# The nine taps of a depthwise convolution divided anew among four engines, and one of its outputs stored turned

## The chip, the core and the metric

The kernel runs on one core of a Trainium2 chip. The core has five engines that each work through their own queue in order: TensorE (PE, matmuls and transposes), VectorE (DVE), ScalarE (ACT), GpSimd (POOL) and SyncE (SP, which here only issues transfers). Transfers run on 16 DMA engines; a transfer is issued by an instruction in the queue of SP or ACT. TensorE writes to PSUM, which ScalarE and VectorE read. The metric is device time in microseconds, the median of several runs.

## What is computed

The reference has two layers over an image x of 256 x 256 tokens with 128 channels. The first is attention along rows; the change doesn't touch it. The second, cut to what matters (g is the group-normalised input, b is 1, the inner width 256, four scan directions k, 16 states):

```python
xz = g @ w_in.T
xi, z = jnp.split(xz, 2, axis=-1)
xc = transpose(xi, (0, 3, 1, 2))
xc = silu(depthwise_conv_3x3(xc, conv_w) + conv_b)
x_flat = xc.reshape(b, d, L)
x_t = transpose(xc, (0, 1, 3, 2)).reshape(b, d, L)
xs = concatenate([[x_flat, x_t], flip([x_flat, x_t])])
x_dbl = einsum('bkdl,kcd->bkcl', xs, x_proj_w)
dts, Bs, Cs = split(x_dbl, [8, 24], axis=2)
ys = selective_scan(xs, dt_w @ dts, -exp(A_logs), Bs, Cs, Ds, dt_b)
out = x + (layernorm(sum of the four directions of ys) * silu(z)) @ w_out.T
```

So for each token the second layer needs nine multiply-adds in each of 256 channels (the depthwise convolution), a silu, and three small projections: the input of the rates and the C of each direction, B of each direction, and the skip product Ds * xs. Directions 1 and 3 go through the image column by column, so they need their rates and C with the image turned.

## The kernel before

The stages run one after the other: `group_stats`, `pair_norm`, `attention`, `conv`, `swap`, `scans`, `output`. Between them everything goes through scratch tensors in DRAM (`mid_...` in the profile). The change lies in `conv` and in the call of `swap`.

`conv` goes over 32 blocks of 8 image rows (2048 tokens). For each block it loads `raw` (10 rows, SP), makes the normalised frame `pad` with a border of zeros (L506, VectorE; borders by GpSimd, L500 to L505), and projects it into `xi`, 256 channels as two halves h of 128 partitions (L522 on TensorE, ten matmuls of 512 columns; L525 copies each from PSUM on ScalarE).

Each block is four chunks q of 512 tokens. For each chunk and half, four of the nine taps (`corners`) are matmuls into one PSUM tile `ps` (L537): the tap's weights are multiplied into the projection `w_in` once, at the start (L475), so that such a tap reads `pad` and not `xi`. The other five taps (`others`) are VectorE operations that multiply a shifted piece of `xi` by a weight for each partition and add what is there already (L547; the first adds to `ps`, the others to `acc`). Then come the sigmoid on ScalarE (L556) and the product of silu on VectorE (L557), which gives `xc`.

From `xc` a chunk makes: `pd` (L560, two matmuls: rates and C of all four directions in 96 rows), copied to `dc` by ScalarE (L563); `pb` (L567, eight matmuls: B), copied to `bk` by VectorE (L570); `pt` (L574, eight transposes: the tokens), copied to `xk` by ScalarE (L575) and multiplied by the skip weights into `y0` by VectorE (L576). `pd`, `pb` and `pt` have one PSUM buffer each, `ps` three, shared with the projections.

At the end of a block, eight stores stand in ScalarE's queue: `xk`, `y`, the two halves of `dc` (`dc1` for the directions that run across, `dc0` for the others), and four of `bk`, one for each direction (L577 to L582). In a store of `bk` each contiguous run is 16 numbers, 64 bytes. The order of the work in `conv` is not written out by hand; a scheduler puts it into the engines' queues.

`swap` then turns `dc1` into `dcT`: two rounds of eight loads (L598, SP), eight copies that exchange the two image axes (L606 on ScalarE, L608 on VectorE) and sixteen stores (L610, ScalarE's queue).

`scans` reads `dc0` for directions 0 and 2, which come first, and `dcT` for directions 1 and 3. For each state and half it runs a scan on VectorE (L858), multiplies the result by C on GpSimd (L861), and does the rest on TensorE and ScalarE. L659 is its first VectorE operation. In `output`, the last stage, GpSimd multiplies two tiles (L1046) while VectorE normalises (L1019, L1023, L1030).

Of the kernel before, what the change touches and what calls it, by code (L numbers as in the profile page):

```python
# [28 lines left out]
F32 = mybir.dt.float32  # L29
# [6 lines left out]
P = 128  # L36
N = 256
# [417 lines left out]
def conv(tc, io, c):  # L455

    nc = tc.nc
# [3 lines left out]
    corners = (0, 2, 6, 8)  # L463
    others = (1, 3, 4, 5, 7)
    with tc.tile_pool(name="d_w", bufs=1) as wp, tc.tile_pool(name="d_in", bufs=2) as inp, tc.tile_pool(
        name="d_sb", bufs=2
    ) as sb, tc.tile_pool(name="d_out", bufs=2) as op, tc.tile_pool(name="d_ps", bufs=3, space=PSUM) as psum, tc.tile_pool(
# [4 lines left out]
        w4 = wp.tile([P, 4, DI], F32, name="w4")  # L472
        for x, t in enumerate(corners):
            nc.sync.dma_start(out=w4[:, x, :], in_=io["conv_wT"][t].partition_broadcast(P))
        nc.vector.tensor_tensor(w4, w4, bcast(win, 1, [P, 4, DI]), ALU.mult)  # L475
# [14 lines left out]
        for b in range(N // R):  # L490
            toks = slice(b * RT, (b + 1) * RT)
            lo, hi = max(b * R - 1, 0), min(b * R + R + 1, N)
            off = lo - (b * R - 1)
            raw = inp.tile([P, R + 2, N], F32, name="raw")
            rows = hi - lo
            nc.sync.dma_start(
                out=raw[:, off : off + rows, :].rearrange("p r w -> p (r w)"), in_=io["x1T"][:, lo * N : hi * N]
            )
            pad = inp.tile([P, R + 2, N + 2], F32, name="pad")
            nc.gpsimd.memset(pad[:, :, 0:1], 0.0)  # L500
            nc.gpsimd.memset(pad[:, :, N + 1 : N + 2], 0.0)
            if off:
                nc.gpsimd.memset(pad[:, 0, :], 0.0)
            if off + rows < R + 2:
                nc.gpsimd.memset(pad[:, R + 1, :], 0.0)  # L505
            nc.vector.tensor_scalar(  # L506
                pad[:, off : off + rows, 1 : N + 1],
                raw[:, off : off + rows, :],
                c.gn2[:, 0:1],
                c.gn2[:, 1:2],  # L510
                ALU.subtract,
                ALU.mult,
            )
            rr = T // N
            xi = inp.tile([P, NH, R + 2, N + 2], F32, name="xi")
            nc.gpsimd.memset(xi[:, :, :, 0:1], 0.0)
            nc.gpsimd.memset(xi[:, :, :, N + 1 : N + 2], 0.0)
            for r in range(0, R + 2, rr):
                for h in range(NH):
                    rows = min(rr, R + 2 - r)  # L520
                    pi = psum.tile([P, T], F32, name="ps").rearrange("p (r w) -> p r w", w=N)[:, 0:rows, :]
                    nc.tensor.matmul(  # L522
                        pi, win[:, h * P : (h + 1) * P], pad[:, r : r + rows, 1 : N + 1], start=True, stop=True
                    )
                    nc.scalar.copy(xi[:, h, r : r + rows, 1 : N + 1], pi)  # L525
            xk = op.tile([P, RT // P, DI], F32, name="xk")
            y0 = op.tile([P, RT // P, DI], F32, name="y0")
            bk = op.tile([P, KD, RT // P, DS], F32, name="bk")
            dc = op.tile([P, RT], F32, name="dc")
            for q in range(RT // T):  # L530
                qs = slice(q * QJ, (q + 1) * QJ)
                xc = sb.tile([P, NH, T], F32, name="xc")
                for h in range(NH):
                    ps = psum.tile([P, T], F32, name="ps")
                    for x, t in enumerate(corners):
                        dy, dx = divmod(t, 3)
                        nc.tensor.matmul(  # L537
                            ps.rearrange("p (r w) -> p r w", w=N),
                            w4[:, x, h * P : (h + 1) * P],
                            pad[:, q * rr + dy : q * rr + dy + rr, dx : dx + N],  # L540
                            start=(x == 0),
                            stop=(x == len(corners) - 1),
                        )
                    acc = sb.tile([P, T], F32, name="acc")
                    for x, t in enumerate(others):
                        dy, dx = divmod(t, 3)
                        nc.vector.scalar_tensor_tensor(  # L547
                            acc.rearrange("p (r w) -> p r w", w=N),
                            xi[:, h, q * rr + dy : q * rr + dy + rr, dx : dx + N],
                            cw[:, t, h : h + 1],  # L550
                            (acc if x else ps).rearrange("p (r w) -> p r w", w=N),
                            ALU.mult,
                            ALU.add,
                        )
                    sg = sb.tile([P, T], F32, name="sg")
                    nc.scalar.activation(sg, acc, AF.Sigmoid, bias=cb[:, h : h + 1])  # L556
                    nc.vector.scalar_tensor_tensor(xc[:, h, :], acc, cb[:, h : h + 1], sg, ALU.add, ALU.mult)  # L557
                pd = pdp.tile([P, T], F32, name="pd")
                for h in range(NH):
                    nc.tensor.matmul(  # L560
                        pd[0 : KD * RC, :], xpc[:, h, :], xc[:, h, :], start=(h == 0), stop=(h == NH - 1)
                    )
                nc.scalar.copy(dc[0 : KD * RC, q * T : (q + 1) * T], pd[0 : KD * RC, :])  # L563
                pb = pdp.tile([P, QJ, KD * DS], F32, name="pb")
                for j in range(QJ):
                    for h in range(NH):
                        nc.tensor.matmul(  # L567
                            pb[:, j, :], xc[:, h, j * P : (j + 1) * P], xpb[:, h, :], start=(h == 0), stop=(h == NH - 1)
                        )
                nc.vector.tensor_copy(bk[:, :, qs, :].rearrange("p k j n -> p j k n"), pb.rearrange("p j (k n) -> p j k n", n=DS))  # L570
                pt = pdp.tile([P, QJ, DI], F32, name="pt")
                for j in range(QJ):
                    for h in range(NH):
                        nc.tensor.transpose(pt[:, j, h * P : (h + 1) * P], xc[:, h, j * P : (j + 1) * P], c.ident)  # L574
                nc.scalar.copy(xk[:, qs, :], pt)  # L575
                nc.vector.tensor_tensor(y0[:, qs, :], pt, bcast(sk, 1, [P, QJ, DI]), ALU.mult)  # L576
            nc.scalar.dma_start(out=io["xk"][toks, :].rearrange("(j p) c -> p j c", p=P), in_=xk)  # L577
            nc.scalar.dma_start(out=io["y"][toks, :].rearrange("(j p) c -> p j c", p=P), in_=y0)
            nc.scalar.dma_start(out=io["dc1"][:, toks], in_=dc[0 : KD // 2 * RC, :])
            nc.scalar.dma_start(out=io["dc0"][:, toks], in_=dc[KD // 2 * RC : KD * RC, :])  # L580
            for k in range(KD):
                nc.scalar.dma_start(out=io["bk"][k, toks, :].rearrange("(j p) n -> p j n", p=P), in_=bk[:, k])  # L582


def swap(tc, io, src, dst):

    nc = tc.nc
    B = 128
    Q = 16
    PR = KD // 2 * RC  # L590
    s = io[src].rearrange("p (i h w) -> i p h w", h=B, w=N)
    d = io[dst].rearrange("p (w i h) -> i p w h", i=N // B, h=B)
    with tc.tile_pool(name=f"s_{dst}", bufs=1) as sb:
        for j in range(N // B):
            a = sb.tile([P, B, B], F32, name="a")
            for i in range(N // B):
                for q in range(0, B, B // 4):
                    nc.sync.dma_start(  # L598
                        out=a[i * PR : (i + 1) * PR, q : q + B // 4, :],
                        in_=s[i, :, q : q + B // 4, j * B : (j + 1) * B],  # L600
                    )
            o = sb.tile([P, B, B], F32, name="o")
            for n, q in enumerate(range(0, B, Q)):
                to, of = o[0 : N // B * PR, q : q + Q, :], a[0 : N // B * PR, :, q : q + Q].rearrange("p h w -> p w h")
                if n % 2:
                    nc.scalar.copy(to, of)  # L606
                else:
                    nc.vector.tensor_copy(to, of)  # L608
# [385 lines left out]
def output(tc, io, c):  # L994
# [70 lines left out]
    "xk": (NT, DI),  # L1065
    "bk": (KD, NT, DS),
    "dc0": (KD // 2 * RC, NT),
    "dc1": (KD // 2 * RC, NT),
    "dcT": (KD // 2 * RC, NT),
    "y": (NT, DI),  # L1070
}
# [58 lines left out]
```

## Time and profile before

| what | us |
|---|---|
| median of three runs | 28848.39 (28846.53 to 28851.29) |
| the profiled execution | 28855.02 |
| its span in the profile | 28853.2 |
| first frame of the convolution, L506 | starts at 2589.9 |
| last skip product of the convolution, L576 | starts at 4562.3 |
| first load and last store of the swap, L598 and L610 | issued at 4582.5 and 4735.5 |
| first scan, L858 | starts at 4784.3 |

| group in the convolution | count | busy us | mean ns |
|---|---|---|---|
| L537 PE tap matmuls | x2048 | 954.9 | 610 |
| L522 PE projections | x640 | 298.0 | 600 |
| L560 PE rates and C | x512 | 302.3 | 689 |
| L567 PE B | x2048 | 260.0 | 274 |
| L574 PE transposes | x1024 | 150.6 | 275 |
| L547 DVE taps, on acc | x1024 | 754.4 | 749 |
| L547 DVE taps, on ps | x256 | 187.9 | 743 |
| L557 DVE silu | x256 | 189.4 | 749 |
| L576 DVE skip product | x128 | 156.3 | 1221 |
| L506 DVE frame | x32 | 53.5 | 1673 |
| L525 ACT copy to xi | x320 | 187.0 | 586 |
| L556 ACT sigmoid | x256 | 181.7 | 721 |
| L575 ACT copy to xk | x128 | 129.5 | 1012 |
| L563 ACT copy to dc | x128 | 74.5 | 582 |

How to read it: a time in the profile counts from the start of the span. L547 is line 547 of the kernel, `acc<-xi,cw,acc` says that the tile `acc` is written from `xi`, `cw` and `acc`. A matmul of 512 columns in float32 has two records. Records on an engine may overlap a little, so the distance from start to start (the pitch) can be shorter than a record. In a wait, "17.58 <-DMA mid_bk<-bk" says that the engine sat idle for 17.58 us until that transfer's issue or end let it go on. The granted clock is the share of full speed that TensorE was given.

### The profile page before, as it was taken

Reading aid. Unit: us, or ns where it says so; the run is one execution under the profiler, and the core shown is the slowest. Engines: PE = TensorE matmul, PEld = TensorE weight load, DVE = VectorE, ACT = ScalarE, POOL = GpSimd, SP = SyncE. Lnnn points to the kernel's source line nnn. Section 1 sums busy time; section 2 is a strip of 40 time slices with the busy share of each in tenths; the row PEclk is TensorE's granted clock in tenths of the full one; section 3 lists DMA queues with packets and bytes.
Section 4 is the critical chain, followed back from the end, with each engine's and each line's share of the span. In section 5 each row is a group of like instructions: output and inputs, shape, how many; then the busy total and the mean of one; then the engine's idle time right before and its main releaser. Section 6 shows DMA issues by size and latency. Waiting matters only on the chain. (4 is left out here: it accounts for less than half of the span.)

```text
span 28853.2 us, 534744 instructions
## 1 busy us (share of the span) xinstructions
PE 26874.7 (93%) x196490; PEld 22493.7 (78%) x196490; DVE 25687.9 (89%) x28349; ACT 25335.6 (88%) x49673; POOL 23024.8 (80%) x10118
## 2 busy tenths in 40 slices
PE   8999996999999999999999999999999999999998
PEld 3555444888888888888888888888888888888884
DVE  4777665999999999999999999999999999999997
ACT  6885225999999999999999999999999999999987
POOL 2442003999999999999999999999999999999983
PEclk9999998999999999999999999999999999999999
DMA  5112444333333333333333333333333333333335
GB/s 204 54 54 70 114 114 115 130 130 128 129 128 130 130 130 130 130 129 130 127 131 130 129 130 130 129 130 127 130 130 130 130 128 129 128 128 130 130 129 173
DMA packets 1924048, 3630.49 MB, mean 126 GB/s; under 512 B 532297, under 2 KB 1240009, under 8 KB 1889490
## 3 DMA queue, kind: packets, MB, share of 16 engines
q1 hardware_dynamic: 1424722, 3339.77, 34.1%
q10 hardware_dynamic: 496640, 255.88, 3.2%
q8 instruction: 1567, 25.67, 0.4%
q14 instruction: 1119, 9.17, 0.1%
HBM read 3002.42 MB, written 592.84 MB: 125 GB/s over the span
## 5 line engine op out<-in xcount | busy, mean ns | idle before, releaser
L861 POOL TENSOR_TENSOR hs<-hs,cc 128x1024 f32<-128x1024 f32 x8192 | 19304.2, 2375 | 1669.6 <-DVE state L860 1178.4
L858 DVE TENSOR_TENSOR_SCAN hs<-da,state,mm 128x1024 f32<-128x1024 f32 x8192 | 19223.4, 2347 | 1026.0 <-PE mm L848 697.5
L846 PE MATMUL mm<-dg,dxt 128*128 128x128 f32 x65536 | 9412.3, 288 | 1260.4 <-DVE hs L858 1023.7
L846 PEld LDWEIGHTS mm<-dg,dxt 128*128 128x128 f32 x65536 | 8243.5, 197 | 2746.4 <-DVE hs L858 2084.1
L839 ACT ACTIVATE da<-delta,A 128x1024 f32<-128x1024 f32 x8192 | 9342.1, 1140 | 93.3 <-PEq L980 65.3
L617 PE MATMUL y<-ident,hs 128*128 128x128 f32 x65536 | 8464.6, 274 | 0.0
L835 ACT ACTIVATE but<-dxt,bt 128x256 f32<-128x256 f32 x16384 | 8172.1, 499 | 11.4 <-DVE dxt L794 11.4
L617 PEld LDWEIGHTS y<-ident,hs 128*128 128x128 f32 x65536 | 7462.6, 142 | 0.2 <-POOL hs L861 0.2
L833 ACT ACTIVATE dg<-ident,bt 128x128 f32<-128x128 f32 x16384 | 6413.3, 391 | 0.2
L848 PE MATMUL mm<-ident,but 128*128 128x128 f32 x32768 | 5089.8, 279 | 0.0
L848 PEld LDWEIGHTS mm<-ident,but 128*128 128x128 f32 x32768 | 4004.3, 146 | 0.0
L750 PE MATMUL mm<-dt,dtw 9*128 9x512 f32 x4096 | 2032.3, 615 | 218.6 <-DMA bt<-mid_bk 183.6
L385 POOL TENSOR_TENSOR an<-ex,rs 128x1024 f32<-128x1024 f32 x512 | 969.6, 1894 | 1029.4 <-PE tp L394 563.1
L860 DVE COPY state<-hs 128x1 f32<-128x1 f32 x8192 | 1259.4, 154 | 280.7 <-DVE hs L858 0.3
L780 POOL TENSOR_TENSOR lw<-lw,e 128x1024 f32<-128x1024 f32 x512 | 1219.9, 2383 | 335.7 <-ACT lw L766 335.7
L750 PEld LDWEIGHTS mm<-dt,dtw 9*128 9x128 f32 x4096 | 680.7, 184 | 916.1 <-issue 723.0
L759 ACT ACTIVATE e<-mm 128x1024 f32<-128x1024 f32 x512 | 524.7, 1025 | 944.8 <-PE mm L750 936.7
L500 POOL MEMSET pad<- 128x10 f32 x32 | 3.7, 117 | 1651.9 <-PE ps L537 1641.8
L777 POOL TENSOR_TENSOR lw<-lw,w 128x1024 f32<-128x1024 f32 x512 | 1216.9, 2377 | 0.0
L537 PE MATMUL ps<-pad,w 128*128 128x512 f32 x2048 | 954.9, 610 | 161.5 <-ACT xi L525 161.5
L372 ACT ACTIVATE ex<-sc,nm 128x256 f32<-128x256 f32 x2048 | 1013.6, 499 | 0.4
L355 DVE CUSTOM_DVE_ANT_0 sc<-ps,bias 128x256 f32<-128x256 f32 x2048 | 746.3, 421 | 119.2 <-PE ps L340 119.2
(137 smaller groups left out, 18393.0 us busy)
## 6 DMA issues: line engine op xcount, KB each, us to landing
cc<-mid_dc SPq DMA_DIRECT2D x2048, 512.0 KB
cc<-mid_dcT SPq DMA_DIRECT2D x2048, 512.0 KB
xk<-mid_xk SPq DMA_DIRECT2D x256, 1024.0 KB
yb<-mid_y SPq DMA_DIRECT2D x256, 1024.0 KB
mid_y<-yb SPq DMA_DIRECT2D x256, 1024.0 KB
xt<-mid_xT SPq DMA_DIRECT2D x64, 1024.0 KB
mid_xk<-xk ACTq DMA_DIRECT2D x32, 2048.0 KB
mid_y<-y ACTq DMA_DIRECT2D x32, 2048.0 KB
```

Of the source, the lines that this page charges most:

```text
L617: nc.tensor.matmul(out, in_, c.ident, is_transpose=True, start=start, stop=stop, skip_group_check=True)
L750: nc.tensor.matmul(pu[:, q : q + T], dtw[0 : DR + 1, k, h * P : (h + 1) * P], B.dt[0 : DR + 1, q : q + T], start=True, stop=True,)
L777: nc.gpsimd.tensor_tensor(B.lw[:, h, :], B.lw[:, h, :], B.w[:, h, :], ALU.add)
L780: nc.gpsimd.tensor_tensor(B.lw[:, h, :], B.lw[:, h, :], B.e[:, h, :], ALU.add)
L833: nc.scalar.activation(dg[:, j, :], c.ident, AF.Copy, scale=B.bt[:, B.slot(j), m : m + 1])
L835: nc.scalar.activation(bu[:, j, :], B.dxt[:, DJ + j, :], AF.Copy, scale=B.bt[:, at, m : m + 1])
L839: nc.scalar.activation(da, B.delta[:, h, :], AF.Exp, scale=A[:, B.S.k * NH + h, m : m + 1])
L846: nc.tensor.matmul(d1[:, j * P : (j + 1) * P], B.dxt[:, j, hc], dg[:, j, :], start=True, stop=True)
L848: nc.tensor.transpose(d1[:, j * P : (j + 1) * P], bu[:, j - DJ, hc], c.ident)
L858: nc.vector.tensor_tensor_scan(o, d0, d1, state[:, m, h : h + 1], ALU.mult, ALU.add)
L860: nc.vector.tensor_copy(state[:, m, h : h + 1], hs[:, h, last : last + 1])
L861: nc.gpsimd.tensor_tensor(hs[:, h, :], hs[:, h, :], ccs[m % 4], ALU.mult)
```

## The change

The nine taps are divided anew: three (`fused`, 0, 8 and 2) stay matmuls; three (`scaled`, 6, 1 and 7) are products on ScalarE, written to tiles `pr` and added up into `acc2` by two GpSimd operations for each chunk and half; three (`others`, 3, 4 and 5) are on VectorE, behind an addition of `ps` and `acc2`.

The order of the work is written out. The work of one step u of the new loop belongs to four chunks: products, matmul taps and sums of chunk u+1; taps, sigmoid and silu of u; silu of the second half, rates, B and transposes of u-1; and the copies and stores of u-2. The projections of the next block are spread over the chunks of this one (0, 4, 3 and 3). They have a PSUM buffer of their own. `raw` has one buffer, `acc`, `acc2`, `sg` and `xc` three, `pr` six.

All stores go into SP's queue. `xk` and `y` are stored for each chunk. The copy of B moves from VectorE to ScalarE. `dc1` and `swap` are gone: ScalarE copies the 48 rows of the directions that run across a second time, with the image axes exchanged, into a tile `dct` that collects 16 image rows, and four stores for each such tile write it to `dcT`; each contiguous run there is 16 numbers, 64 bytes.

```diff
@@ conv
-    corners = (0, 2, 6, 8)
-    others = (1, 3, 4, 5, 7)
...
+    fused = (0, 8, 2)
+    scaled = (6, 1, 7)
+    others = (3, 4, 5)
...
+        def project(b, n):
+            r, h = parts[n]
+            rows = min(rr, R + 2 - r)
+            pi = lines(pdp.tile([P, T], F32, name="pi"))[:, 0:rows, :]
+            nc.tensor.matmul(
+                pi, win[:, h * P : (h + 1) * P], pads[b][:, r : r + rows, 1 : N + 1], start=True, stop=True
             )
...
+            nc.scalar.copy(xis[b][:, h, r : r + rows, 1 : N + 1], pi)
...
+        def products(u, h):
+            xi = xis[u // QB][:, h]
+            prods[u, h] = []
+            for t in scaled:
+                pr = prp.tile([P, T], F32, name="pr")
+                nc.scalar.activation(lines(pr), shifted(xi, u, t), AF.Copy, scale=cw[:, t, h : h + 1])
+                prods[u, h].append(pr)
+
+        def sums(u, h):
+            acc2 = acc2s[u, h] = sb.tile([P, T], F32, name="acc2")
+            first, *others = prods.pop((u, h))
+            for pr in others:
+                nc.gpsimd.tensor_tensor(acc2, first, pr, ALU.add)
+                first = acc2
+
+        def taps(u, h):
+            xi = xis[u // QB][:, h]
+            acc = accs[u, h] = sb.tile([P, T], F32, name="acc")
+            nc.vector.tensor_tensor(acc, pss.pop((u, h)), acc2s.pop((u, h)), ALU.add)
+            for t in others:
+                nc.vector.scalar_tensor_tensor(
+                    lines(acc), shifted(xi, u, t), cw[:, t, h : h + 1], lines(acc), ALU.mult, ALU.add
+                )
...
+        def save_rates(u):
+            pd = pds.pop(u)
+            toks = slice(u * T, (u + 1) * T)
+            dc = op.tile([P, T], F32, name="dc")
+            nc.scalar.copy(dc[0 : KD * RC, :], pd[0 : KD * RC, :])
+            nc.sync.dma_start(out=io["dc0"][:, toks], in_=dc[KR : 2 * KR, :])
+
+            g, q = divmod(u, 2 * QB)
+            if q == 0:
+                dcs[g] = op.tile([P, N, 2 * R], F32, name="dct")
+            nc.scalar.copy(dcs[g][0:KR, :, q * rr : (q + 1) * rr].rearrange("p w r -> p r w"), lines(pd[0:KR, :]))
+            if q == 2 * QB - 1:
+                to = io["dcT"].rearrange("p (w h) -> p w h", h=N)[:, :, g * 2 * R : (g + 1) * 2 * R]
+                of = dcs.pop(g)
+                for w in range(0, N, N // 4):
+                    nc.sync.dma_start(out=to[:, w : w + N // 4, :], in_=of[0:KR, w : w + N // 4, :])
...
+        def save_tokens(u):
+            xk = op.tile([P, QJ, DI], F32, name="xk")
+            nc.scalar.copy(xk, pts[u])
+            nc.sync.dma_start(out=io["xk"][u * T : (u + 1) * T, :].rearrange("(j p) c -> p j c", p=P), in_=xk)
+
+        def save_skip(u):
+            y0 = op.tile([P, QJ, DI], F32, name="y0")
+            nc.vector.tensor_tensor(y0, pts.pop(u), bcast(sk, 1, [P, QJ, DI]), ALU.mult)
+            nc.sync.dma_start(out=io["y"][u * T : (u + 1) * T, :].rearrange("(j p) c -> p j c", p=P), in_=y0)
...
+            for u in range(-1, K + 2):
...
+                if q == 0:
+                    framed(b + 1)
+                    load(b + 2)
+                when(products, u + 1, 0)
+                when(corners, u + 1, 0)
+                when(sums, u + 1, 0)
+                when(save_rates, u - 2)
+                when(taps, u, 0)
+                some()
+                when(sigmoid, u, 0)
+                when(silu, u - 1, NH - 1)
+                when(corners, u + 1, 1)
+                when(save_bs, u - 2)
+                when(save_tokens, u - 2)
+                when(save_skip, u - 2)
+                some()
+                when(products, u + 1, 1)
+                when(sums, u + 1, 1)
+                when(taps, u, 1)
+                when(rates, u - 1)
+                some(9)
+                when(silu, u, 0)
+                when(sigmoid, u, 1)
+                when(bs, u - 1)
+                when(turned, u - 1)
+                if q == 0:
+                    opened(b + 1)
...
@@ build
     conv(tc, io, c)
-    swap(tc, io, "dc1", "dcT")
     scans(tc, io, c)
```

K is 128, the number of chunks; QB is 4, the chunks of a block; `when` leaves out chunks that don't exist. `framed` makes `pad` as before, `load` and `opened` load `raw` and zero the borders of `xi`, `some(n)` does up to n projections of the next block, and `corners`, `sigmoid`, `silu`, `rates`, `bs` and `turned` do what the same work did before.

## The prediction

> **What bounds the kernel now.** I first read the stretches of the span, cut at three instructions: the first frame of the convolution (L506, 2589.9 us), the end of its last skip product (L576, 4563.5) and the first scan (L858, 4784.3). Columns: stretch, length, busy time of TensorE, its weight loads, VectorE, ScalarE and GpSimd, granted clock, DMA share, GB/s.
>
> ```profile
> 2589.90:4563.50 1973.60, 1800.58 (x6272) 949.91 (x6272) 1354.27 (x1826) 560.67 (x833) 10.63 (x121) 0.94 0.39 108
> 4563.50:4784.30 220.80, 23.06 (x56) 13.04 (x56) 20.82 (x17) 52.55 (x44) 9.26 (x4) 0.52 0.88 156
> ```
>
> The convolution takes 1973.6 us: 128 chunks of 512 tokens, 15.42 us each, TensorE busy 91% of it, ScalarE 28%, GpSimd idle. Then 220.8 us pass in which only DMA is busy: the swap. The scans (23,286 us) and the rest stay as they are. Next, the timeline around one block's end, for what breaks TensorE's run:
>
> ```profile
> 3512.79 13.90 PE L537 MATMUL ps<-pad,w 128*128 128x512 f32 x32
> ...
> 3516.56 14.11 ACTq L582 DMA_DIRECT2D mid_bk<-bk  x4
> ...
> 3517.28 3.18 DVE L547 SCALAR_TENSOR_TENSOR acc<-xi,cw,acc 128x512 f32<-128x512 f32 x4
> ...
> 3530.72 0.59 ACT L525 COPY xi<-ps 128x512 f32<-128x512 f32 x1 [17.58 <-DMA mid_bk<-bk]
> ...
> 3531.36 2.07 PE L537 MATMUL ps<-pad,w 128*128 128x512 f32 x2 [4.67 <-ACT xi L525]
> ```
>
> ScalarE issues four transfers for 14 us and computes nothing; TensorE waits 4.67 us for its copy, then runs at half speed (a matmul is two records: 0.87 us before, 2.07 after) for some 7 us (to 3538.5). The view of waits counts 549.6 us of such ScalarE time in 31 blocks. Prices come from the groups (last fields: busy us, mean ns) and from single lines:
>
> ```profile
> L861 POOL TENSOR_TENSOR hs<-hs,cc 128x1024 f32<-128x1024 f32 x8192 | 19304.2, 2375 | 1669.6 <-DVE state L860 1178.4
> ...
> L839 ACT ACTIVATE da<-delta,A 128x1024 f32<-128x1024 f32 x8192 | 9342.1, 1140 | 93.3 <-PEq L980 65.3
> ...
> L835 ACT ACTIVATE but<-dxt,bt 128x256 f32<-128x256 f32 x16384 | 8172.1, 499 | 11.4 <-DVE dxt L794 11.4
> ```
> ```profile
> L659 DVE MEMSET dt<- x1: 912/912/912, 4741.1 to 4741.1; 9x1024 f32 x1
> ```
>
> The second is the first VectorE work behind the swap, 43 us before the first scan.
>
> **The swap goes.** Of the 220.8 us, 19 are the drain of the last transfers (to 4582.5, where the swap's first load issues), 158.6 the swap to 4741.1, 43.2 the scans' lead-in. The new conv writes dcT itself, so drain and lead-in stay; the drain grows by the last dcT transfers, 7.7 us by the price below: 19 + 8 + 43 = 70, a gain of 150 (140 if those packets cost four times as much). The scans read the same layout, so they are charged nothing.
>
> **TensorE.** Matmul pitch 13.90/16 = 0.87 us. A chunk before: 8 tap matmuls, 2.5 projections and 2 rate matmuls make 10.9, the B products 1.7 (1.51 us for 14 records), the transposes 0.9: 13.5, at clock 0.94 14.3 (measured 14.07). One tap fewer in each half takes off 1.74: 11.7 us.
>
> **ScalarE.** Six scaled taps are new. L835 (256 elements, 499 ns) and L839 (1024, 1140 ns) give 0.71 us at 512 and, since successive ones start 0.10 us before the last ends, a pitch of 0.61: 3.7 us. The old copies and sigmoids cost 573 us over 128 chunks, 4.5 each. The B copy moves here (0.4), and a second, strided copy of the rates is added: 0.58 (L563) to 0.91 (a quarter of L606's strided 3642 ns for 2048 elements). Sum 9.2 to 9.5 us, below TensorE, so it costs only through order. All DMA issues leave this queue, so the 17 us holes and the half-clock spells behind them go.
>
> **SP's queue** takes them: in eight chunks 8 dc0, 8 xk, 8 y, 8 bk, 4 dcT and 2 raw loads; an issue is 0.3 to 0.9 us when nothing is backed up, some 20 us per 116. Behind a waiting SP stand only later stores and the next raw load, which is due four chunks later. The transfers themselves: B's 8192 packets of 64 B move in 6.2 us at a DMA share of 0.82, 10 ns a packet and engine. dcT is also 64 B runs, 12288 packets per eight chunks, scattered 1 KB apart: 7.7 us at 10 ns; at the 39 ns of the swap's 512 B packets (24,576 in 29.8% of 16 engines' 200 us), 30 us. I take 10, the row of its own packet size. A burst of dcT, B, xk and y is then 17 us; ScalarE's xk copy two chunks (29 us) later waits for that buffer, so it is hidden; at 39 ns the burst is 39 and 10 us show per group of eight, 16 x 10 = 160 us.
>
> **VectorE and GpSimd.** Per half VectorE now has one add of PSUM and acc2 (L1051: 0.68), then three dependent taps at a pitch of 0.79 (3.18 us for four), with no wait for GpSimd in the ordinary case, as acc2 is made one chunk ahead: 3.0 us, where five taps took 3.9. With silu (0.7 twice), skip product (1.22) and pad (0.4) that is 9.1 us. GpSimd gets four adds of 128x512; half of L861 is 1.19 us, 4.8 in all.
>
> What an add does to a tap that runs beside it is not in this trace, since no VectorE operation with two SBUF streams meets GpSimd. The two nearest rows lie in the output stage:
>
> ```profile
> 28404.08 2.44 POOL L1046 TENSOR_TENSOR yz<-yz,z 128x1024 f32<-128x1024 f32 x1 [4.56 <-ACT yz L1043]
> 28404.22 2.85 DVE L1019 TENSOR_SCALAR xn<-xt,gn 128x1024 f32<-128x1024 f32 x1
> ...
> 28409.89 0.75 DVE L1023 BATCH_NORM_STATS2 st<-y 128x6 f32<-128x256 f32 x2 [0.60 <-DMA y<-mid_y]
> 28409.96 2.36 POOL L1046 TENSOR_TENSOR yz<-yz,z 128x1024 f32<-128x1024 f32 x1 [3.43 <-ACT yz L1043]
> ```
>
> L1019, SBUF to SBUF, has a median of 0.81 us and took 2.85 beside GpSimd: it stood until GpSimd had nearly ended (2.05 of 2.44 us lost). L1023, one stream in and six numbers out, was not delayed. So an add costs VectorE between 0 and about 1.1 us. I take 1.1: the tap moves whole tiles from SBUF to SBUF, as L1019 does.
>
> The Trainium skill ("SBUF — State Buffer", section "Who interferes with whom") speaks against the change here: it says that a VectorE instruction with two SBUF inputs contends with a GpSimd instruction that reads SBUF, the later one blocking fully. L1019 agrees for another kind of operation; the case itself no run here shows. By the rule the blocked sum below holds, without it the unblocked one.
>
> **The loop that sets the chunk.** TensorE's 11.7 us would set it, but the written order ties two engines: sigmoid(u,0) waits for taps(u,0); on ScalarE the xk copy stands behind that sigmoid; the skip product of the same PSUM tile waits for that copy (it did before: L576 behind L575); taps(u,1) stand behind the skip product, sigmoid(u,1) behind them, and the next chunk's scaled taps behind that. From the end of one taps(.,1): silu and the add to 1.4, a tap to 2.1, an add of GpSimd (its products are ready at 2.0) to 3.2, tap 4.0, GpSimd 5.1, tap 5.9; ScalarE has been ready since 4.4 (its strided copy is hidden by 1.4 us here), sigmoid, B copy and xk copy to 7.9; skip product 9.2, add 9.8, tap 10.6, and again two blocked taps to 14.3. A chunk that opens a block has the pad (1.6) and no projection copies: 15.1. Mean 14.5. Unblocked the same walk gives 10.7 and TensorE rules: 11.7, at uneven projections (0, 4, 3, 3 per chunk) some 12.1.
>
> **Sum.** 128 x 14.5 = 1856, plus 35 of filling and emptying (ten projections through one PSUM buffer at 1.6 each, a first chunk of 7 us, two last ones of 6 and 4, 2 for the frame): 1891, against 1973.6: -83. With the swap -233. The profiled span is 28853.2 us, its run 28855.0, the median 28848.4; I take it from the median: 28615.
>
> **Rivals.** *Unblocked taps* (22%): 128 x 12.1 + 35 = 1584, -390 - 150: 28308. For it: L1023 and the scans, where L858 and L861 run side by side at their own pace (but L858 has one input in PSUM). Against it: L1019. *The turned store is dear* (8%): blocked taps plus 160 us of late xk buffers, -73: 28775. For it: scattered 64 B runs, the swap's slow packets; against: B's own packets. *Slower: TensorE loses its clock in every chunk* (8%). The place is the wait of the rate matmuls for silu and of the transposes for the skip product. If that gap reaches the 4.67 us of the row above, 7 us run at half speed, TensorE needs 11.7 + 3.5 and the gap, some 19.9 in all: 128 x 19.9 + 35 = 2582, +608 - 150: 29307. It decides from a chunk of 16.3 us on, where (2124 - 35)/128 just eats the swap's gain. Against: TensorE idles 2.8 us per blocked chunk in total (5.6 in one of four). That the swap's time does not go is excluded, since no instruction of it is left.
>
> **How the numbers follow.** Blocked taps have 62%; their own range, 13.8 to 15.3 us per chunk (add at 0.95 to 1.3 us, queue handovers of 0.05 to 0.1 us that the walk leaves out), is 28520 to 28720. To leave out no more than 2 in 10 the range takes in the unblocked case and the dear store: 28300 to 28780. A measurement of this kernel tells about 0.2%, 58 us, from no change. Faster by more: 62 + 22, of which nothing lies above 28790: 0.84. The dear store straddles that line: same 0.08. Slower 0.08.
>
> **What would show it.** Right: no DMA issue on ScalarE and no swap; the first scan near 4550; L591's mean near 1.3 us against 0.75 with records long just where L583 runs; TensorE about 80% busy in the conv. L591 at 0.75 makes the unblocked case. The xk copy (L665) waiting on its own transfers makes the dear store; matmuls at 2.07 us per pair in every chunk make the slower one. I am wrong if VectorE wins the port and GpSimd's adds slide into its waits, which would bring the chunk back near 12 us.

## The result and the profile after

| | before | after |
|---|---|---|
| median of four runs | 28849.84 us (28846.53 to 28852.13) | 28496.55 us (28465.53 to 28526.60) |
| profiled execution, and its span | 28855.02, 28853.2 | 28465.53, 28463.7 |
| convolution, first frame to end of last skip product | 1973.6 | 1786.0 |
| end of last skip product to first scan | 220.8 | 62.5 |

The ratio is 0.9878, 95% interval 0.9865 to 0.9890. The two stages that the change touches give 187.6 + 158.3 = 346 us of the 353 between the medians. The profiled execution of after is the fastest of its four: it also spends 42 us less in the scans (23239.9 against 23281.9 before), where the code doesn't differ.

The same two stretches as before, in the windows view of after (columns as in the prediction: stretch, length, busy time of TensorE, weight loads, VectorE, ScalarE, GpSimd, granted clock, DMA share, GB/s):

```profile
2588.50:4374.50 1786.00, 1584.05 (x5760) 823.70 (x5760) 1551.91 (x1442) 1150.34 (x1857) 743.61 (x635) 0.98 0.46 121
4374.50:4437.00 62.50, 23.98 (x56) 13.69 (x56) 6.08 (x7) 23.29 (x36) 9.25 (x4) 0.51 0.47 107
```

The granted clock of the convolution rose from 0.94 to 0.98: most of the half-speed time is gone (the clock records of the two traces have 226 us of it in this stage before and 87 here). But TensorE is now busy only 89% of the time, and VectorE, at 1552 us, carries more than before (1354), although each half lost two VectorE taps and got one addition for them. The timeline of one chunk shows why:

```profile
3509.75 0.74 DVE L602 SCALAR_TENSOR_TENSOR xc<-acc,cb,sg 128x512 f32<-128x512 f32 x1
3509.86 0.72 ACT L597 ACTIVATE sg<-acc,cb 128x512 f32<-128x512 f32 x1 [1.50 <-DVE acc L591]
...
3510.41 0.68 DVE L589 TENSOR_TENSOR acc<-ps,acc 128x512 f32<-128x512 f32 x1
...
3511.13 4.26 DVE L591 SCALAR_TENSOR_TENSOR acc<-xi,cw,acc 128x512 f32<-128x512 f32 x3
...
3511.89 1.27 POOL L583 TENSOR_TENSOR acc<-pr 128x512 f32<-128x512 f32 x1 [3.40 <-ACT pr L576]
...
3513.24 1.60 POOL L583 TENSOR_TENSOR acc<-acc,pr 128x512 f32<-128x512 f32 x1
...
3515.43 0.72 ACT L597 ACTIVATE sg<-acc,cb 128x512 f32<-128x512 f32 x1 [1.02 <-DVE acc L591]
...
3516.05 0.35 ACT L653 COPY bk<-pb 128x256 f32<-128x256 f32 x1
...
3516.31 1.01 ACT L665 COPY xk<-pt 128x1024 f32<-128x1024 f32 x1
...
3517.35 1.22 DVE L670 TENSOR_TENSOR y<-pt,sk 128x1024 f32<-128x1024 f32 x1 [1.30 <-ACT xk L665]
```

Three taps (L591) take 4.26 us, where three that run undisturbed take 2.33 (a row of `taps_psum` below). Two additions of GpSimd lie inside them. ScalarE's sigmoid waits for the taps, the copy to `xk` stands behind the sigmoid, and VectorE's skip product waits for the copy. The next half's taps are queued behind that product. The groups of after (last fields: busy us, mean ns) and its waits in the convolution (total us, times, longest us) put numbers to it:

```profile
L591 DVE SCALAR_TENSOR_TENSOR acc<-xi,cw,acc 128x512 f32<-128x512 f32 x768 | 1015.2, 1322 | 27.3
...
L583 POOL TENSOR_TENSOR acc<-acc,pr 128x512 f32<-128x512 f32 x256 | 407.6, 1592 | 20.1
...
L583 POOL TENSOR_TENSOR acc<-pr 128x512 f32<-128x512 f32 x256 | 327.5, 1279 | 968.2 <-ACT pr L576 962.9 <-DVE y L670 5.4
```
```profile
ACT sg L597 <- DVE acc L591: 546.9, 250, 4.6
...
DVE y L670 <- ACT xk L665: 176.7, 128, 5.6
```

A tap's median is 1639 ns and its shortest 750: most are held, some not at all. The 506 taps that ran beside an addition took 1617 ns on average, the other 262 took 752. GpSimd's first addition has a median of 1270 ns, the second 1596, so each engine holds the other up. So far this is a reading; the runs below test it.

### The profile page after: what moved, and what is told of

Its sections match the earlier page's. It is cut to its first block, busy times and chain, and to the rows that moved or that the text cites. A ratio compares the mean times of both kernels' runs of the same rounds, so it can differ in the third digit from the quotient of the medians.

```text
span 28463.7 us, 535680 instructions
## 1 busy us (share of the span) xinstructions
PE 26611.0 (93%) x195978; PEld 22317.5 (78%) x195978; DVE 25869.1 (91%) x27957; ACT 25894.5 (91%) x50689; POOL 23752.8 (83%) x10630
## 5 line engine op out<-in xcount | busy, mean ns | idle before, releaser
L583 POOL TENSOR_TENSOR acc<-pr 128x512 f32<-128x512 f32 x256 | 327.5, 1279 | 968.2 <-ACT pr L576 962.9
L591 DVE SCALAR_TENSOR_TENSOR acc<-xi,cw,acc 128x512 f32<-128x512 f32 x768 | 1015.2, 1322 | 27.3
```

## The experiments

Each is an edit of after unless it says "before". "Convolution" is the stretch of the table above, in the profiled execution; medians are over four runs, or five where it says so. "Ratio" is the time over that of before, run beside it, with its 95% interval. The cuts of code show what matters of each edit; `...` stands for the rest.

**Is it the addition that holds the taps?** In `taps_psum` the taps add to the PSUM tile in place, and `acc2` comes last, so no tap has two SBUF inputs:

```diff
-            nc.vector.tensor_tensor(acc, pss.pop((u, h)), acc2s.pop((u, h)), ALU.add)
+            ps = pss.pop((u, h))
             for t in others:
                 nc.vector.scalar_tensor_tensor(
-                    lines(acc), shifted(xi, u, t), cw[:, t, h : h + 1], lines(acc), ALU.mult, ALU.add
+                    lines(ps), shifted(xi, u, t), cw[:, t, h : h + 1], lines(ps), ALU.mult, ALU.add
                 )
+            nc.vector.tensor_tensor(acc, ps, acc2s.pop((u, h)), ALU.add)
```

> Edit: VectorE's three taps accumulate in the PSUM tile ps, and the addition of acc2 comes last and writes acc. Same work; no tap has two SBUF streams any more, only xi comes from SBUF. Theory (a GpSimd addition that reads SBUF holds a tap with two SBUF streams): the taps go back from a mean of 1.32 us to 0.75 to 0.80, a chunk falls from 13.7 us to between 12.1 and 12.7 and is then set by TensorE, the conv from 1786 to about 1620, the time to about 28330. Rival (the taps are long for some other reason, or the loop through the xk copy sets the chunk anyway): taps stay near 1.3 us or the conv stays within 30 us of 1786, time 28470 to 28530.

Measured: 28334.06 us (28329.58 to 28343.16), ratio 0.9822 [0.9805, 0.9838], convolution 1618.8. The timeline of `taps_psum`:

```profile
3512.03 2.33 DVE L591 SCALAR_TENSOR_TENSOR ps<-xi,cw,ps 128x512 f32<-128x512 f32 x3
...
3512.16 1.27 POOL L583 TENSOR_TENSOR acc<-pr 128x512 f32<-128x512 f32 x1 [3.81 <-DVE y L671]
...
3513.51 1.27 POOL L583 TENSOR_TENSOR acc<-acc,pr 128x512 f32<-128x512 f32 x1
...
3518.16 0.69 DVE L594 TENSOR_TENSOR acc<-ps,acc 128x512 f32<-128x512 f32 x1
...
3518.57 1.27 POOL L583 TENSOR_TENSOR acc<-acc,pr 128x512 f32<-128x512 f32 x1
...
3518.77 1.61 DVE L603 SCALAR_TENSOR_TENSOR xc<-acc,cb,sg 128x512 f32<-128x512 f32 x1
```

With one input in PSUM, three taps run in 2.33 us beside two additions, and these additions too keep their 1.27. Silu, which still has both inputs in SBUF, started 0.20 us after an addition and took 1.61 us instead of 0.74: the same instruction form is held or not by where its operands lie. The edit moved the taps' output to PSUM as well, but the output isn't what matters: the last addition (L594) reads one input from PSUM, writes to SBUF, and takes 691 to 693 ns in all 256 cases, also beside GpSimd. Silu's mean is 1090 ns here (754 in after), and the additions' means are 1386 and 1493. Moving the taps away takes 167 us off the convolution.

One input in SBUF is not safe for every operation. The frame (L529, a tensor_scalar from SBUF to SBUF) has a median of 2656 ns here, where in 30 of 32 cases an addition had begun some 0.6 us before it, and 1608 in after, where none had.

The Trainium skill ("SBUF — State Buffer", section "Who interferes with whom") says this of two SBUF inputs beside a GpSimd instruction that reads SBUF, and that a VectorE instruction with at most one SBUF input, outside its two-port modes, does not contend. The taps agree: mean 1322 ns against 753.

`no_sums` leaves out the additions instead, and with them two of the three products from the result (bufs of `pr` raised from 6 to 9 so that nothing new waits):

```diff
-            acc2 = acc2s[u, h] = sb.tile([P, T], F32, name="acc2")
-            first, *others = prods.pop((u, h))
-            for pr in others:
-                nc.gpsimd.tensor_tensor(acc2, first, pr, ALU.add)
-                first = acc2
+            acc2s[u, h] = prods.pop((u, h))[-1]
```

> Edit: GpSimd's additions are left out, and with them two of the three scaled taps (the third product alone is added); ScalarE still makes all three. Theory of the held taps: L591 at 0.75 us, chunk about 12.1 (TensorE's 11.7 and its uneven projections), conv near 1590 to 1620, time 28300 to 28330, the unblocked sum of the prediction. Rival: the loop sets the chunk, conv above 1750.

Measured: 28292.37 us (28285.13 to 28313.04), ratio 0.981 [0.9794, 0.9827], convolution 1555.9, mean tap 752 ns, TensorE busy 1518.9 us of it (98%):

```profile
2589.40:4145.30 1555.90, 1518.94 (x5760) 833.67 (x5760) 1111.41 (x1442) 1156.51 (x1857) 10.66 (x121) 0.98 0.54 139
```

So without the hold TensorE sets the chunk, at 1518.9 / 128 = 11.9 us. The convolution came out 34 us below the expected range and the time 8 us below: the unheld chunk is TensorE's own, with nothing added for uneven projections.

`three_six` gives the three scaled taps to VectorE: three matmuls, six VectorE taps, no products, no GpSimd.

```diff
-    others = (3, 4, 5)
+    others = (6, 1, 7, 3, 4, 5)
...
-                when(products, u + 1, 0)
...
-                when(sums, u + 1, 0)
...
```

> Edit: three taps stay fused, the other six are all on VectorE; no products on ScalarE, no additions on GpSimd. Same order otherwise. VectorE has 12.3 us a chunk. Theory with the loop through xk and the skip product: taps(u,0) 4.7 after silu 0.7, sigmoid, B and xk copies to 7.4, skip product 8.7, taps(u,1) to 13.3: conv 35 + 128 x 13.3 = 1737, time about 28450. Without that loop (rival) VectorE's own 12.3 us: conv 1610, time 28320.

Measured: 28499.49 us (28475.75 to 28518.65), ratio 0.9879 [0.9862, 0.9895], convolution 1769.1, 32 us more than expected (the time 49 us more). VectorE computes 1511 us and waits 181.7 us for the copy to `xk`. Within the spread of the runs it is as fast as after: the two additions, with the hold they bring, cost VectorE as much as the three taps that they save it.

**What were the single parts worth?** `before_sp` is before with one edit: the eight stores of a block go from ScalarE's queue to SP's.

```diff
-            nc.scalar.dma_start(out=io["xk"][toks, :].rearrange("(j p) c -> p j c", p=P), in_=xk)
+            nc.sync.dma_start(out=io["xk"][toks, :].rearrange("(j p) c -> p j c", p=P), in_=xk)
...
```

> Edit: the kernel before with nothing changed but the stores of the conv, which SP issues instead of ScalarE. Theory (the 17 us holes in ScalarE and the half-clock spells behind them are most of what the conv lost over TensorE's own 13.5 us a chunk): conv from 1974 to between 1780 and 1840, swap as before, time 28660 to 28720. Rival (the holes only move to waits for buffers that are not yet stored): conv above 1930, time above 28800.

Measured: 28601.23 us (28591.65 to 28619.63), ratio 0.9916 [0.9899, 0.9932], 59 us below the expected range. The windows view of `before_sp`:

```profile
2586.40:4312.70 1726.30, 1714.70 (x6272) 919.63 (x6272) 1363.10 (x1826) 558.73 (x833) 10.59 (x121) 0.99 0.45 123
```

TensorE is busy 99% of the stretch at a clock of 0.99. The whole convolution gained 247 us, and it is now 60 us shorter than that of after: the 17 us of stores in ScalarE's queue at each block's end, and the half-clock spells behind them, were all that kept this stage from TensorE's own time.

`before_turned` adds the turned store to `before_sp` (the `dct` tile, its copy and four stores as in after, no swap, one buffer of `raw`), but leaves division and order as they were:

```diff
+                nc.scalar.copy(
+                    dct[0:KR, :, at : at + rr].rearrange("p w r -> p r w"), pd[0:KR, :].rearrange("p (r w) -> p r w", w=N)
+                )
...
-    swap(tc, io, "dc1", "dcT")
...
```

> Edit: the kernel before with its own order and division of taps, the conv's stores issued by SP, the rates across stored turned by a second ScalarE copy and four stores for each 16 rows, the swap gone; raw has one buffer to make room. Theory (the queue and the swap are separate gains, and the new order and division add nothing to them): conv as with the stores on SP alone, about 1722, way to the first scan about 65: 28601 - 155, time 28430 to 28470, thus below the changed kernel's 28496. Rival (the new order is needed to hide the turned copy and its stores): conv above 1780, time above 28500.

Measured: 28474.79 us (28462.01 to 28489.13), ratio 0.9876 [0.9860, 0.9892], convolution 1733.7, then 74.2 to the first scan (each some 10 us more than expected, and the time 5 us above its range):

```profile
2585.50:4319.20 1733.70, 1718.67 (x6272) 916.91 (x6272) 1353.04 (x1826) 672.22 (x961) 10.59 (x121) 0.99 0.48 123
4319.20:4393.40 74.20, 22.65 (x56) 12.37 (x56) 6.08 (x7) 23.30 (x36) 9.26 (x4) 0.52 0.55 133
```

That is as fast as after (the ranges overlap), with none of its new division and order.

`old_division` keeps the new order and stores of after, but takes four taps as matmuls and five on VectorE, with no products and no additions:

```diff
-    fused = (0, 8, 2)
+    fused = (0, 8, 2, 6)
-    others = (3, 4, 5)
+    others = (1, 7, 3, 4, 5)
...
```

> Edit: the old division of taps (four fused, five on VectorE) in the new written order, stores and dcT as in the changed kernel. TensorE 13.4 us a chunk, 13.6 to 13.8 with uneven projections, VectorE's loop 11.7. Theory (the new division of taps gives back in held taps what it takes off TensorE, and the gain in the conv comes from the order and the queue): conv 1770 to 1820, time within 0.15% of the changed kernel, 28460 to 28540. Rival (the division is what gains): slower by one matmul tap per half, 1.74 x 128 = 220, time about 28720.

Measured: 28482.22 us (28479.85 to 28503.80), ratio 0.9876 [0.9860, 0.9893], convolution 1774.3: as expected, under this order the new division brings nothing that can be seen.

`swap_back` is after with `dc1` and `swap` again instead of the turned store:

```diff
...
+            nc.sync.dma_start(out=io["dc1"][:, toks], in_=dc[0:KR, :])
...
+    swap(tc, io, "dc1", "dcT")
...
```

> Edit: the changed conv, but the rates of the directions across are stored as dc1 again and the old swap turns them; the strided second copy on ScalarE and the four dcT stores go. Theory (two separate gains, about 158 us of swap and about 188 of conv): the way from the last skip product to the first scan goes from 62.5 us to about 215, the conv stays near 1786 since the strided copy lies in ScalarE's wait for the taps, the time rises by about 150 to 28645. Rival (the 64-byte stores and the strided copy cost the conv something): conv shorter by 30 us or more, the time rises by less than 120.

Measured: 28660.09 us (28646.75 to 28670.75), ratio 0.9934 [0.9918, 0.9951], 164 us above after. Convolution 1785.0, then 212.6 to the first scan: the turned store costs this convolution nothing.

`stores_act` puts the stores of after's convolution into ScalarE's queue:

```diff
-            nc.sync.dma_start(out=io["y"][u * T : (u + 1) * T, :].rearrange("(j p) c -> p j c", p=P), in_=y0)
+            nc.scalar.dma_start(out=io["y"][u * T : (u + 1) * T, :].rearrange("(j p) c -> p j c", p=P), in_=y0)
...
```

> Edit: the changed kernel with all stores of the conv issued from ScalarE's queue instead of SP's. Theory (the queue matters: ScalarE stands while a full queue takes the issues, about 16 us in a chunk with dcT and B, 7 in one with B alone, of which some 4 lie in its slack): 16 x 12 + 16 x 3 = 240 us more, time 28650 to 28800. Rival (issues cost nothing, as ScalarE has room): within 40 us of 28496.

Measured: 28950.63 us (28944.74 to 28970.90, five runs), ratio 1.0037 [1.0023, 1.0051]: slower than before, and 150 us above the expected range. The convolution takes 2260.2 us at a granted clock of 0.84. ScalarE and its queue (ACTq) in the timeline:

```profile
3502.14 1.01 ACT L665 COPY xk<-pt 128x1024 f32<-128x1024 f32 x1
3503.18 0.38 ACTq L666 DMA_DIRECT2D mid_xk<-xk  x1
3504.44 0.38 ACTq L671 DMA_DIRECT2D mid_y<-y  x1
3504.87 1.95 ACT L576 ACTIVATE pr<-xi,cw 128x512 f32<-128x512 f32 x3 [1.72 <-DVE y L670]
...
3533.02 0.59 ACT L553 COPY xi<-pi 128x512 f32<-128x512 f32 x1 [4.76 <-PE pi L550]
...
3534.52 4.45 ACTq L661 DMA_DIRECT2D mid_bk<-bk  x4
3539.01 1.01 ACT L665 COPY xk<-pt 128x1024 f32<-128x1024 f32 x1 [4.52 <-issue]
```

What the expectation had left out: the store of `y` waits in ScalarE's queue for VectorE's skip product, in every chunk, and copies and products stand idle behind it (1.72 us in the fourth row). Before had such stores only at a block's end. Waits of ScalarE on the skip product sum to 204 us (153.9 before L553, 49.8 before L576); behind its own issues and their transfers it stood some 300 us (138.0 before L553, 161.7 before L665), and the clock was lower. How the 474 us by which this convolution is longer than that of after divide between the three was not separated, so what made the miss is argued, not shown.

**Is it a loop?** `skip_first` exchanges two lines, so that the skip product no longer waits for the copy to `xk`:

```diff
-                when(save_tokens, u - 2)
                 when(save_skip, u - 2)
+                when(save_tokens, u - 2)
...
```

> Edit: in the changed kernel the skip product is put ahead of the xk copy in the written order, so VectorE no longer waits there for ScalarE behind the sigmoid. Theory (held taps and the loop through the xk copy set the chunk together): the 177 us that the skip product waited go, the second half's taps run before GpSimd's additions of that half, chunk 12.2 to 13.1, time 28300 to 28420. Rival (the lock alone, however it is ordered, sets the chunk): chunk stays at 13.5 or more, time 28470 to 28530.

Measured: 28253.80 us (28242.94 to 28262.84), ratio 0.9795 [0.9778, 0.9811], 243 us below after and 46 below the expected range. The groups of `skip_first` within the convolution, and its windows view:

```profile
L591 DVE SCALAR_TENSOR_TENSOR acc<-xi,cw,acc 128x512 f32<-128x512 f32 x768 | 774.4, 1008 | 27.4
...
L597 ACT ACTIVATE sg<-acc,cb 128x512 f32<-128x512 f32 x256 | 185.0, 723 | 16.0 <-DVE acc L591 12.5
```
```profile
2586.40:4142.20 1555.80, 1518.44 (x5760) 832.76 (x5760) 1396.35 (x1442) 1154.99 (x1856) 750.03 (x635) 0.98 0.54 139
```

The additions are all there and still hold taps (mean 1008 ns), yet the convolution is as long as without them (1555.9). ScalarE's waits before the sigmoid fell from 546.9 to 16.0 us. Part of the hold went with the new order too: half of the taps run free now (median 752 ns against 1639), while silu is held in their place (mean 1073 ns against 754), and VectorE's busy time fell from 1552 to 1396 us. So the hold cost time because VectorE and ScalarE waited for each other by turns; with one of the two waits gone, what is left of it fits under TensorE, which is busy 98% of the stretch. `skip_psum` makes both edits, `skip_first` and `taps_psum`:

> Edit: skip product ahead of the xk copy, and the taps accumulate in PSUM. Theory (with the skip product first TensorE sets the chunk and the held taps, 1.0 us in the mean, are hidden): conv near 1555 as with the first edit alone, time 28235 to 28275. Rival (held taps still cost): conv shorter by 30 us or more, time below 28225.

Measured: 28279.68 us (28259.52 to 28286.47), ratio 0.9804 [0.9788, 0.9821], convolution 1549.0, mean tap 753 ns: the two gains do not add, since the second removes what the first had already hidden. With the second edit alone (1618.8) the loop still cost 70 us. The time lies 5 us above the expected range and 26 above `skip_first`, though the convolution is 7 us shorter; the difference lies in the scans, which neither edit touches.

**What does the stage allow?** With TensorE as the bound, a tap less for it should count at last. `two_three_four` and `two_four` are `skip_psum` with two fused taps; the third goes to VectorE or to ScalarE and GpSimd (there with eight buffers of `pr`):

```diff
-    fused = (0, 8, 2)
+    fused = (0, 8)
...
-    others = (3, 4, 5)
+    others = (2, 3, 4, 5)
```
```diff
-    fused = (0, 8, 2)
-    scaled = (6, 1, 7)
+    fused = (0, 8)
+    scaled = (2, 6, 1, 7)
```

> Edit: as the kernel with both edits, but two taps are matmuls, three products on ScalarE, four on VectorE in PSUM. TensorE 10.0, ScalarE 9.4, VectorE 10.7, GpSimd 5.1 us a chunk. Theory: VectorE then sets it, 10.9 to 11.4 with what is held of its silu, conv 1430 to 1490, time 28120 to 28190. Rival as for the other division: chunk 11.7 or more, time above 28230.

Measured: 28186.43 us (28184.40 to 28189.92), ratio 0.9774 [0.9758, 0.9790], convolution 1474.3.

> Edit: as the kernel with both edits, but two taps are matmuls, four are products on ScalarE with three GpSimd additions, three on VectorE in PSUM. TensorE 10.0 us a chunk, ScalarE 10.6, VectorE 9.1, GpSimd 7.6. Theory (TensorE sets the chunk in the kernel with both edits): the chunk falls with it until ScalarE is as long, 10.6 to 11.2, conv 1390 to 1470, time 28080 to 28170. Rival (something else is as long, VectorE's silu held by longer GpSimd work or the loop): chunk 11.7 or more, time above 28230.

Measured: 28119.17 us (28093.28 to 28121.69), ratio 0.9749 [0.9732, 0.9765], the fastest version, 377 us below after. The windows view of `two_four`:

```profile
2588.80:3981.20 1392.40, 1305.65 (x5248) 734.02 (x5248) 1210.37 (x1442) 1279.63 (x2112) 1026.60 (x891) 0.98 0.60 156
```

TensorE, ScalarE and VectorE now carry 1306, 1280 and 1210 us of 1392: no engine has much left to take from another.

## Why the prediction was right, and where its size was off

**The swap.** Predicted −150, measured −158.3. Drain 19.3 and lead-in 43.2 came as the trace of before had them; the 8 us put on for the last `dcT` transfers did not show.

**The held taps.** The choice of the blocked case was right: `taps_psum` and `no_sums` show the cause. The reason given for it, that the tap moves whole tiles from SBUF to SBUF, was not the one that counts: L594 of `taps_psum` moves a whole tile from SBUF to SBUF too, with its other input in PSUM, and is not held. The mean tap of 1322 ns meets the "near 1.3" by luck, since the prediction's own walk has three taps in 4.5 us, 1.5 each.

**The loop, and the term that was mis-sized.** The walk can be laid beside the timeline, from the end of one taps(.,1), at 3509.83, to the next, at 3523.43:

| stretch of the walk | predicted | measured |
|---|---|---|
| silu and addition | 1.4 | 1.30 |
| three taps, first half | 4.5 | 4.26 |
| sigmoid, copies of B and `xk` | 2.0 | 1.93 |
| skip product and addition | 1.9 | 1.89 |
| three taps, second half | 4.5 | 4.22 |
| an ordinary chunk | 14.3 | 13.60 |
| a chunk that opens a block | 15.1 | 13.87 |

The term "I take 1.1" (an addition's cost to a tap) was too large. Held taps take 4.2 us for 2.33, so an addition costs (4.2 − 2.33) / 2 = 0.94; by the mean record (1322 − 749) × 3 / 2 = 0.86 us, since GpSimd itself is held in its second addition and some taps meet none. In a chunk that opens a block the frame (1.6 us) goes ahead of the first taps, the additions begin under it, and the taps took only 3.53 and 3.70 us. Held taps therefore make 0.52 us of an ordinary chunk's error and 1.77 of an opening one's: 96 × 0.52 + 32 × 1.77 = 107 us, against an error of 1891 − 1786 = 105. That these agree is partly luck: the walk's other terms were 0.18 us too long in an ordinary chunk and 0.54 too short in an opening one, 17 us each way. The forecast of 28615 lay 118 us above the result; 8 of the rest are the swap's.

The result also lies 24 us below the range that the prediction gave to blocked taps (28520 to 28720, at 13.8 to 15.3 us a chunk, where 13.6 was measured). It is inside the stated 28300 to 28780 because that was widened to take in the unblocked taps.

**TensorE.** 11.7 us a chunk was foreseen, `skip_first` and `no_sums` show 11.9. "About 80% busy" was wrong: it was 89%, for a shorter chunk and because its records are longer in a broken run (L563 608 ns on average here, 594 in `skip_first`).

**ScalarE, and the stores.** A load of 9.2 to 9.5 us was foreseen, 1150.3 / 128 = 9.0 measured; a scaled tap costs 715 ns where 0.71 us was estimated, the strided copy of the rates 1036 ns where at most 0.91 was. It is hidden all the same. What the prediction treated as a side effect, the stores' move to SP's queue, is the largest part: 249 us alone (`before_sp`, against 28849.84). It was inside the new chunk's sum and had no term of its own.

**The rivals.** The copy to `xk` waited 0.6 us in all, so the dear store did not occur. The unblocked case, with 12.1 us a chunk, was a fair picture of another kernel: `no_sums` gives 11.9 and 28292 us for a forecast of 28308. The half clock in every chunk did not come (0.98 was granted), but a kernel like that exists: in `stores_act` TensorE waits up to 5.3 us at a time and is granted 0.84, at (2260 − 35) / 128 = 17.4 us a chunk, beyond the 16.3 that the rival named.

**Where the gain came from.** Stores in SP's queue −249, and no swap −126 to −164 (`before_turned` against `before_sp`; after against `swap_back`): together more than the whole change, so that the new division and the new order brought nothing on balance (the order with the old division: a convolution of 1774.3 in `old_division` against 1733.7 in `before_turned`). The tap taken from TensorE in each half, 196 us of its busy time against `before_sp` by `skip_first` (1714.7 − 1518.4), was given back on VectorE and in the loop, and came out only once two lines were exchanged.

## What to carry to other kernels

Work taken from the engine that sets the time can be worth nothing if the written order makes two other engines wait for each other by turns: walk the order round once, from an instruction to its own next occurrence, and look first for two readers of one PSUM tile that follow each other. When GpSimd is given sums, see that VectorE's work beside them has at most one input in SBUF, or has slack, and look at operations like the frame apart: it was held with one. Before a stage is rebuilt, take the waiting stores out of a computing engine's queue; here that one edit gave 249 of 353 us.

## What the runs showed of the hardware that was not expected

The hold goes both ways and is not lost time by itself: the same additions cost the convolution 230 us in after (against `no_sums`) and nothing that shows in `skip_first` (1555.8 us against 1555.9). A copy of 48 rows with exchanged axes takes ScalarE 1036 ns, the plain one of 96 rows 562. The runs of after spread by 61 us (granted clock 0.973 to 0.977) but by 6 in the first four runs of before; the further runs of before, beside the experiments, went from 28811.75 to 28878.66, so one close set of four says little of the next.
